# A two-layer transformer kernel: the order of its first stage, where its zero-fills start, and where the row that every token gets is added

## Chip, cores and metric

One NeuronCore of a Trainium2 chip runs the whole program. The metric is the time of one execution in microseconds (us) on the device; lower is better.

## What is computed

Two layers over x, 2 sequences of 2048 tokens with 256 features, in 32-bit floats. Layer 0, the part that the change touches, is

```
xn = layernorm(x)
x  = x + attention(xn, Wq,bq, Wk,bk, Wv,bv)        # causal, one head, softmax(q k^T / 16) v
       + shared(xn)                                # mean of 2 SwiGLU experts, biases sb1, sb2, sb3
       + routed(xn)                                # softmax gate (gate_w, gate_b), top 2 of 8 SwiGLU experts
```

Layer 1 has a second causal attention and a small 16-head block on the 256 highest-scoring tokens of each sequence. The change does not edit layer 1's computation.

Two facts carry the algebra at the start. The queries and keys are never formed separately: `wa` = Wq^T Wk is built once, and a score is xn · wa · xn^T plus terms from the biases. Of those, the key-side term is a vector `ca` added to the projected query, the query-side term is one number per row (`shift`) and bq·bk is one constant. Constants per row do not alter a softmax, but the kernel carries them. And the row `every` = (sb3[0]+sb3[1])/2 + bv is the same for all tokens, since the softmax weights sum to one and the shared experts are averaged.

## The kernel before

**Tiles.** Tokens lie in eight blocks of 512 (`x_blocks[g]`, 4 groups of 128 tokens). Blocks 0 to 3 are sequence 0. Attention goes over tiles of 128 queries, (0,0) to (0,15) upwards and then sequence 1 from tile 15 down. Tile i looks at i+1 groups of 128 keys, in chunks of up to 512.

**One attention tile.** `scores` (L251) multiplies on TensorE into PSUM; VectorE adds the mask (L260), adds the row shift and takes the maximum (L262, L268); ScalarE takes the exponential (L270). `turn` splits the row into two 16-bit planes on GpSimd (L301) and sends them through a transposing DMA on SP's queue (L303, `across`). `join` puts the halves together on VectorE (L281) and ScalarE (L282) as `pT`. `average` multiplies with the values (L316) and VectorE adds the result to x (L326). There are two `row` buffers, four each of `planes` and `across`, six `pT`, and two PSUM banks each for `sc`, `tr`, `mm`, `pv`.

**Work beside it.** A generator `side0` yields small steps that are woven between attention's pieces at a rate: `moments` (means and variances by L201, L202, and a reciprocal root by Newton steps, L185 to L190), `prepare0` (normalised rows on ScalarE, L223; transposes, L229, into `xnT`; 16-bit `rows` for the router, L472; the add of `every` to the block on GpSimd, L474; values, gate logits and shift in one product, L481), then the routing. `before_tile` forces steps until the tile's values exist, and issues zero-fills (`clear_some`, L420 onwards: scratch areas `sorted_x`, `sorted_y`, `gains`, 13 + 1 + 8 large DMAs, then biases) on ScalarE's queue. Before the first tile, the moments and `prepare0` of block 0 run whole.

**The beginning.** SP's queue loads all eight x blocks; ScalarE's queue loads wq, wk, bq, bk, wv, gate_w; GpSimd's queue loads gate_b and the three rows of `every`. TensorE turns wq and wk (L375), ScalarE copies them out (L376), then come ten products for the bias terms (L399, L404) and the four for `wa` (L457); `project_q0` (L594) makes a block's queries.

**Routed part.** 36 tiles of 256 sorted tokens. Per tile SP's queue loads the expert's w1, w2, w3 (`rw`, L684) and biases (`be`, L688) and a transposed `xs` (L693); GpSimd turns xs into `xT` (L698); TensorE does L705 into `sc` and `tr`, ScalarE and VectorE make `hid` (L713, L714, which need `be`), TensorE does L720 (needs w3), VectorE adds the bias (L725), SP stores (L726). Weights, `be` and `xs` have two buffers, `xT` three.

**What sets the order.** Each engine and each DMA queue works through its own list strictly in order. The lists are fixed beforehand by a planner that knows estimated durations; the code gives data dependencies and some order-only edges (`tc.add_manual_dep`). What a queue's front instruction waits for, everything behind it waits for as well.

Of the kernel before, what the change touches and what calls it, by code (L numbers as in the profile page):

```python
# [46 lines left out]
def transformer_kernel(ctx: ExitStack, tc: tile.TileContext, a: dict, out: bass.AP):  # L47
# [27 lines left out]
    for g in range(NB):  # L75
        load_x(g, nc.sync)
# [69 lines left out]
    def evacuate(dst, src):  # L146

        copies[0] += 1
        if copies[0] % 2:
            nc.vector.tensor_copy(dst, src)  # L150
        else:
            nc.scalar.copy(dst, src)

    def column(name, n, tag):
        t = const.tile([P, n], F32, tag=tag, name=tag)
        nc.scalar.dma_start(t, a[name])
        return t
# [35 lines left out]

    def moments(blocks):
# [3 lines left out]
        for k, g in enumerate(blocks):  # L198
            stats = small.tile([P, 4, 6], F32, tag="ln_stats", name="ln_stats")
            for j in range(4):  # L200
                nc.vector.bn_stats(stats[:, j, :], x_blocks[g][:, j, :])  # L201
                nc.vector.bn_aggr(mv[:, 4 * k + j, :], stats[:, j, :])  # L202
            if g != blocks[-1]:
                yield
# [11 lines left out]
    scaled = {}  # L216

    def layernorm(g, xn):

        xb = x_blocks[g]  # L220
        rstd, shift = scaled[g]
        for j in range(4):
            nc.scalar.activation(  # L223
                xn[:, j, :D], xb[:, j, :], AF.Identity, bias=shift[:, j : j + 1], scale=rstd[:, j : j + 1]
            )
        for c in range(2):
            ps = bank("mm")
            for j in range(4):
                nc.tensor.transpose(ps[:, j * P : (j + 1) * P], xn[:, j, c * P : (c + 1) * P], ident)  # L229
            evacuate(xnT[g][:, c, :], ps)  # L230
# [129 lines left out]
    with ExitStack() as l0:  # L360
# [6 lines left out]
        wq, wk = (work.tile([P, S], F32, tag="row", name=n)[:, : 2 * D].rearrange("p (c n) -> p c n", c=2)  # L367
                  for n in ("wq", "wk"))
        for dst, name in ((wq, "wq0"), (wk, "wk0")):
            turned = weight(work, name, "qT")  # L370
            ps = bank("mm")
            for ec in range(2):
                for dc in range(2):
                    k = (2 * ec + dc) * P
                    nc.tensor.transpose(ps[:, k : k + P], turned[:, dc, ec * P : (ec + 1) * P], ident)  # L375
            nc.scalar.copy(dst, ps.rearrange("p (c n) -> p c n", c=2))  # L376
        bq = column("bq0", 2, "bq0")
        bk = column("bk0", 2, "bk0")
        wvg = weight(wpool, "wv0", "wvg", cols=D + E + 1)
        nc.scalar.dma_start(wvg[:, :, D : D + E], a["gate_w"].rearrange("(c p) n -> p c n", p=P))  # L380
        gate_b = row_broadcast(wpool, ["gate_b"], "gate_b")


        every = wpool.tile([P, 1, D], F32, tag="every", name="every")
        parts = work.tile([P, 4, D], F32, tag="xn", name="parts", bufs=1)
        for k, src in enumerate((a["sb3"][0], a["sb3"][1], a["bv0"])):
            nc.gpsimd.dma_start(parts[:, k, :], src.partition_broadcast(P))
        nc.gpsimd.tensor_tensor(every[:, 0, :], parts[:, 0, :], parts[:, 1, :], ALU.add)
        nc.gpsimd.tensor_scalar(every[:, 0, :], every[:, 0, :], 0.5, None, op0=ALU.mult)
        nc.gpsimd.tensor_tensor(every[:, 0, :], every[:, 0, :], parts[:, 2, :], ALU.add)  # L390
        wa = wpool.tile([P, 2, D], F32, tag="wa", name="wa")
        ca = wpool.tile([P, 2], F32, tag="ca", name="ca")
        qk_bias = wpool.tile([P, 1], F32, tag="qk_bias", name="qk_bias")
        ps = bank("mm")
        for c in range(2):
            at = slice(c * P, (c + 1) * P)
            for k, (w, v) in enumerate(((wk, bq), (wq, bk))):
                for ec in range(2):
                    nc.tensor.matmul(  # L399
                        ps[:, 2 * k + c : 2 * k + c + 1], lhsT=w[:, ec, at], rhs=v[:, ec : ec + 1],  # L400
                        start=(ec == 0), stop=(ec == 1),
                    )
        for ec in range(2):
            nc.tensor.matmul(  # L404
                ps[:, 4:5], lhsT=bq[:, ec : ec + 1].to_broadcast([P, P]), rhs=bk[:, ec : ec + 1],
                start=(ec == 0), stop=(ec == 1),
            )
        nc.vector.tensor_scalar(ca, ps[:, 0:2], 1.0 / 16.0, None, op0=ALU.mult)
        nc.vector.tensor_scalar(wvg[:, :, D + E], ps[:, 2:4], 1.0 / 16.0, None, op0=ALU.mult)
        nc.vector.tensor_scalar(qk_bias, ps[:, 4:5], 1.0 / 16.0, None, op0=ALU.mult)  # L410

# [41 lines left out]

        for dc in range(2):
            ps = bank("mm")
            for ec in range(2):
                nc.tensor.matmul(  # L457
                    ps[:, :D], lhsT=wq[:, ec, dc * P : (dc + 1) * P], rhs=wk[:, ec, :],
                    start=(ec == 0), stop=(ec == 1),
                )  # L460
            evacuate(wa[:, dc, :], ps[:, :D])
        logits = plan.tile([P, NB * 4, E], F32, tag="logits", name="logits")
        rows, values, shifts = [None] * NB, [None] * NB, [None] * NB

        def prepare0(g):
# [3 lines left out]
            rows[g] = rows_pool.tile([P, 4, 2 * D], U16, tag=f"rows{g}", name=f"rows{g}")  # L469
            halves = xn.bitcast(U16).rearrange("p j (d k) -> p j d k", k=2)  # L470
            for k in range(2):
                nc.gpsimd.tensor_copy(rows[g][:, :, k * D : (k + 1) * D], halves[:, :, :, 1 - k])  # L472
            yield
            nc.gpsimd.tensor_tensor(  # L474
                x_blocks[g], x_blocks[g], every[:, 0:1, :].to_broadcast([P, 4, D]), ALU.add
            )
            vg = kv.tile([P, 4, D + E + 1], F32, tag=f"vg{g}", name=f"vg{g}")
            for j in range(4):
# [6 lines left out]
                evacuate(vg[:, j, :], ps[:, : D + E + 1])  # L485
                yield
            values[g] = vg
            shifts[g] = kv.tile([P, 4], F32, tag=f"shift{g}", name=f"shift{g}")
            nc.vector.tensor_scalar(shifts[g], vg[:, :, D + E], qk_bias, None, op0=ALU.add)
            nc.vector.tensor_tensor(  # L490
                logits[:, 4 * g : 4 * g + 4, :], vg[:, :, D : D + E],
                gate_b.unsqueeze(1).to_broadcast([P, 4, E]), ALU.add,
            )
# [107 lines left out]
        def side0():  # L601
            for blocks in (range(1, BPB), range(BPB, NB)):
                yield from moments(blocks)
                for g in blocks:
                    yield from prepare0(g)
# [3 lines left out]
        def before_tile(b, i):  # L609
            while values[b * BPB + i // 4] is None:  # L610
                step()
            rate[0] = BESIDE_L0[(values[BPB - 1] is not None) + (values[NB - 1] is not None)]
            if (b, i) > (0, 0):
                clear_some(2 if i < 8 and b == 0 else 1)

        for work_of in (moments([0]), prepare0(0)):
            for _ in work_of:
                pass
# [53 lines left out]
    with ExitStack() as moe:  # L672
# [55 lines left out]

        coming = later_weights()
        for t in range(LIKELY):  # L730
            product, activated = run(t)
            if t >= LIKELY // 3:
# [17 lines left out]
    ln1, ln2 = column("ln1", 2, "ln1"), column("ln2", 2, "ln2")  # L750
# [720 lines left out]
```

## Time and profile before

| what | us |
|---|---|
| three runs | 1544.1, 1547.49, 1548.82; median 1547.49 |
| profiled execution | 1543.37 |
| its span (first to last instruction) | 1541.7 |
| around the span | 1.67 |
| TensorE matmul busy | 1478.2 (96%) |
| VectorE, ScalarE, GpSimd busy | 697.3 (45%), 442.0 (29%), 410.2 (27%) |
| first score product | starts at 33.40 |
| first product with values | starts at 55.57 |
| routing's product L537 | starts at 131.97 |
| first routed product L705 | starts at 360.08 |

Stages: start and layer 0's attention to 360 us, routed experts to about 735, shared experts to about 1140 with the selected tokens of sequence 0 beside them, layer 1's attention to the end. TensorE's share says where the bound is, but not what a microsecond of one stage is worth: its busy time is modelled from starts and includes products that run at a lower clock. A gap in its list, or a stretch where the same product takes twice as long, is what can be won or lost.

### The profile page before, as it was taken

What the parts mean: (1) busy time and instruction counts of PE and PEld (TensorE: products, weight loads), DVE (VectorE), ACT (ScalarE), POOL (GpSimd) and SP (SyncE); (2) the same over time, 40 slices, a digit from 0 to 9 for tenths busy, and PEclk for the clock granted to TensorE, in tenths of its full rate; (3) what the DMA queues carried; (4) which work ended last, traced back from release to release, by engine and by line L of the source; (5) the groups of instructions that cost most, each with busy time, mean ns of one, the idle gap of its engine ahead of it and who ended that gap; (6) DMA issues with size and microseconds to landing.
All of it is one profiled execution on the core that took longest, in us unless ns stands there. A gap on an engine that the chain in (4) does not pass through costs nothing.

```text
span 1541.7 us, 17887 instructions
## 1 busy us (share of the span) xinstructions
PE 1478.2 (96%) x5828; PEld 1050.5 (68%) x5828; DVE 697.3 (45%) x2055; ACT 442.0 (29%) x831; POOL 410.2 (27%) x596
## 2 busy tenths in 40 slices
PE   7999899998999999999999999999999998999998
PEld 4566566567888888888565565566675765577665
DVE  6346333343222222222244445866546468666354
ACT  2443233242111111111112212114633532344233
POOL 3554577532111111110122210231003213421132
PEclk9899999999999999999999999999999999999999
DMA  4844556666879888965001110040004425621144
GB/s 152 255 109 120 135 139 138 149 138 150 209 215 226 239 234 256 261 189 158 28 28 41 42 34 21 28 150 18 11 11 92 115 67 106 165 57 23 29 119 102
DMA packets 290558, 183.49 MB, mean 119 GB/s; under 512 B 192960, under 2 KB 265408, under 8 KB 290464
## 3 DMA queue, kind: packets, MB, share of 16 engines
q1 hardware_dynamic: 255168, 134.95, 36.0%
q10 hardware_dynamic: 27664, 26.53, 5.6%
q0 software_dynamic: 7632, 20.86, 4.4%
q8 instruction: 47, 0.77, 0.2%
q14 instruction: 47, 0.39, 0.1%
HBM read 93.14 MB, written 45.14 MB: 90 GB/s over the span
## 4 chain that ended last, share of the span: by engine, by line
PE 28%; issue 10%; DVE 7%; POOL 3%; DMA 2%; ACT 2%; SPq 0%; POOLq 0%; ACTq 0%; DVEq 0%
PE ps_tr L1338 6%; PE ps_sc L1338 6%; PE ps_pv L1357 5%; POOL planes L301 3%; DMA across<-planes 2%; PE ps_mm L1209 1%; PE ps_mm L1171 1%; DVE x L1368 1%; PE ps_sc L251 1%; PE ps_mm L801 1%; PE ps_mm L1192 1%; PE ps_pv L316 1%; PE ps_mm L1275 1%; DVE row L262 1%; ACT pr L1183 1%
## 5 line engine op out<-in xcount | busy, mean ns | idle before, releaser
L301 POOL COPY planes<-row 128x512 uint16<-128x512 uint16 (+3 forms) x320 | 167.7, 569 | 306.8 <-ACT row L270 293.8
L282 ACT COPY pT<-across 128x512 uint16<-128x512 uint16 (+3 forms) x160 | 106.3, 677 | 226.9 <-DMA across<-planes 211.7
L251 PE MATMUL ps_sc<-xnT,qT 128*128 128x512 f32 (+3 forms) x384 | 161.2, 541 | 0.3 <-DVE qT L150 0.2
L714 DVE SCALAR_TENSOR_TENSOR hid<-ps_tr,be,act 128x256 f32<-128x256 f32 x144 | 63.0, 479 | 197.9 <-PE ps_tr L705 192.9
L713 ACT ACTIVATE act<-ps_sc,be 128x256 f32<-128x256 f32 x144 | 60.4, 470 | 302.1 <-PE ps_sc L705 302.1
L1327 POOL DMA_INDIRECT ya<-sorted_y,place x64 | 62.2, 973 | 318.0 <-DVE x L1368 224.9
L316 PE MATMUL ps_pv<-vg,pT 128*128 128x256 f32 x544 | 129.0, 390 | 12.4 <-ACT pT L282 12.0
L705 PE MATMUL ps_sc<-xT,rw 128*128 128x256 f32 x576 | 136.2, 379 | 1.6 <-POOL xT L698 1.6
L705 PE MATMUL ps_tr<-xT,rw 128*128 128x256 f32 x576 | 136.1, 379 | 0.0
L316 PE MATMUL ps_pv<-v,pT 128*128 128x256 f32 x544 | 128.4, 381 | 7.0 <-ACT pT L282 4.6
L720 PE MATMUL ps_pv<-rw,hid 128*128 128x256 f32 x576 | 132.0, 382 | 0.0
L698 POOL COPY xT<-xs 128x512 uint16<-128x512 uint16 x72 | 51.3, 758 | 299.8 <-issue 281.9
L316 PEld LDWEIGHTS ps_pv<-vg,pT 128*128 128x128 f32 x544 | 104.6, 195 | 37.6 <-ACT pT L282 17.5
L1338 PE MATMUL ps_sc<-xnT,sw 128*128 128x512 f32 x256 | 121.9, 594 | 0.1
L1338 PE MATMUL ps_tr<-xnT,sw 128*128 128x512 f32 x256 | 122.0, 593 | 0.0
L316 PEld LDWEIGHTS ps_pv<-v,pT 128*128 128x128 f32 x544 | 101.3, 190 | 29.1 <-ACT pT L282 7.9
L705 PEld LDWEIGHTS ps_sc<-xT,rw 128*128 128x128 f32 x576 | 109.4, 190 | 16.8 <-POOL xT L698 2.0
L705 PEld LDWEIGHTS ps_tr<-xT,rw 128*128 128x128 f32 x576 | 109.5, 190 | 14.8
L720 PEld LDWEIGHTS ps_pv<-rw,hid 128*128 128x128 f32 x576 | 105.0, 190 | 21.2 <-DVE hid L714 6.7
L1357 PE MATMUL ps_pv<-sw,hid 128*128 128x256 f32 x512 | 117.5, 380 | 0.0
L1357 PEld LDWEIGHTS ps_pv<-sw,hid 128*128 128x128 f32 x512 | 96.6, 190 | 18.7 <-issue 6.2
L281 DVE COPY pT<-across 128x512 uint16<-128x512 uint16 (+3 forms) x160 | 68.8, 436 | 89.2 <-DMA across<-planes 88.3
(319 smaller groups left out, 1936.7 us busy)
## 6 DMA issues: line engine op xcount, KB each, us to landing
rw<-in_rw SPq DMA_DIRECT2D x108, 512.0 KB, 4.6
sorted_x<-zero ACTq DMA_DIRECT2D x13, 768.0 KB, 6.6
sorted_y<-y SPq DMA_DIRECT2D x36, 256.0 KB, 4.8
be<-biases SPq DMA_DIRECT2D x36, 132.0 KB, 4.5
table<-xn SPq DMA_DIRECT2D x8, 514.0 KB, 3.7
x<-in_x SPq DMA_DIRECT2D x8, 512.0 KB, 6.8
gains<-zero ACTq DMA_DIRECT2D x8, 512.0 KB, 3.2
gain<-gains SPq DMA_DIRECT2D x16, 256.0 KB, 2.7
```

Source lines behind the costliest of these rows:

```text
L251: product = nc.tensor.matmul(ps[:, :w], lhsT=qT[:, dc, (i % 4) * P : (i % 4 + 1) * P], rhs=xnT[g0 + k][:, dc, :w], start=(dc == 0), stop=( ...
L281: nc.vector.tensor_copy(words[:, :, 1], flat[:, :w]),
L282: nc.scalar.copy(words[:, :, 0], flat[:, w : 2 * w]),
L301: nc.gpsimd.tensor_copy(planes[:, h * w : (h + 1) * w], halves[:, :, 1 - h])
L316: product = nc.tensor.matmul(pv[:, :D], lhsT=turned[k][:, j : j + P], rhs=values[g0 + k][:, j // P, :D], start=(c + j == 0), stop=(c + j = ...
L705: nc.tensor.matmul(ps[:, k * TT : (k + 1) * TT], lhsT=we_in[:, dc, (h + k) * P : (h + k + 1) * P], rhs=xT[:, dc, :], start=(dc == 0), stop ...
L713: activated = nc.scalar.activation(act, p1[:, at], AF.Silu, bias=b1[:, hc])
L714: nc.vector.scalar_tensor_tensor(hid[:, h + k, :], p2[:, at], b2[:, hc], act, op0=ALU.add, op1=ALU.mult)
L720: product = nc.tensor.matmul(po[:, r, :], lhsT=hid[:, hc, r * P : (r + 1) * P], rhs=w3[:, hc, :], start=(hc == 0), stop=(hc == 3),)
L1327: nc.gpsimd.indirect_dma_start(out=ya, out_offset=None, in_=sorted_y, in_offset=bass.IndirectOffsetOnAxis(ap=place[rank][:, t : t + 1], ax ...
L1338: product = nc.tensor.matmul(ps, lhsT=ww[:, dc, hc * P : (hc + 1) * P], rhs=xnT[g][:, dc, :], start=(dc == 0), stop=(dc == 1),)
L1357: product = nc.tensor.matmul(po[:, :D], lhsT=hid[:, hc, j * P : (j + 1) * P], rhs=w["sw3", n][:, hc, :], start=(hc == 0), stop=(hc == 3),)
```

## The change

It reorders the beginning. SP's queue loads block 0, then wk, then the other blocks; wq and wv go on ScalarE's queue, bk, bq and gate_b on GpSimd's (and layer 1's ln1, ln2). bk lands as a 257th column of the turned wk, so that the product `wa` yields the query-side bias column too. A tiny exponential is issued early on ScalarE. The first block's moments go ahead of the other blocks' on VectorE, and half of its normalised rows are made on VectorE. The ten bias products become five, behind `wa`. `gate_b` and bq·bk are added to the values' tail in place.

Block 0's values are no longer finished before the first tile: tile i waits for group i of its values only (`made`), so scores go between them. Other blocks' moments run as side steps that stay behind attention's own work. The zero-fills start at tile 4 (two per tile to tile 11, then one) in place of tile 1.

The add of `every` leaves `prepare0` (eight GpSimd instructions of 128x1024) and enters the routed part (32 of 128x256, written one per tile from tile 4), with its three loads and three small sums.

The core of the diff:

```diff
-    for g in range(NB):
-        load_x(g, nc.sync)
+    load_x(0, nc.sync)
...
             for j in range(4):
-                nc.vector.bn_stats(stats[:, j, :], x_blocks[g][:, j, :])
+                i = nc.vector.bn_stats(stats[:, j, :], x_blocks[g][:, j, :])
+                if first:
+                    tc.add_manual_dep(i.ins, first[0].name, order, reason="the first block's norm goes first")
                 nc.vector.bn_aggr(mv[:, 4 * k + j, :], stats[:, j, :])
+                if j == 1 and g >= BPB:
+                    yield HOLD
             if g != blocks[-1]:
-                yield
+                yield HOLD
...
+            if alone and j % 2:
+                nc.vector.tensor_scalar(
+                    xn[:, j, :D], xb[:, j, :], rstd[:, j : j + 1], shift[:, j : j + 1], op0=ALU.mult, op1=ALU.add
+                )
...
+        nc.gpsimd.dma_start(wk[:, :, D], a["bk0"])
+        bq = column("bq0", 2, "bq0", nc.gpsimd)
+        loaded = [weight(work, n, "qT", queue) for n, queue in (("wq0", nc.scalar), ("wk0", nc.sync))]
+        wvg = weight(wpool, "wv0", "wvg", cols=D + E + 1)
+        for g in range(1, NB):
+            load_x(g, nc.sync)
+
+        warm = const.tile([P, 1], F32, tag="warm", name="warm")
+        nc.vector.memset(warm, 0.0)
+        nc.scalar.activation(warm, warm, AF.Exp)
+        for _ in moments([0]):
+            pass
...
-        every = wpool.tile([P, 1, D], F32, tag="every", name="every")
-        parts = work.tile([P, 4, D], F32, tag="xn", name="parts", bufs=1)
-        for k, src in enumerate((a["sb3"][0], a["sb3"][1], a["bv0"])):
-            nc.gpsimd.dma_start(parts[:, k, :], src.partition_broadcast(P))
...
-                    ps[:, :D], lhsT=wq[:, ec, dc * P : (dc + 1) * P], rhs=wk[:, ec, :],
+                    ps[:, : D + 1], lhsT=wq[:, ec, dc * P : (dc + 1) * P], rhs=wk[:, ec, :],
...
             layernorm(g, xn)
-            rows[g] = rows_pool.tile([P, 4, 2 * D], U16, tag=f"rows{g}", name=f"rows{g}")
...
-            yield
-            nc.gpsimd.tensor_tensor(
-                x_blocks[g], x_blocks[g], every[:, 0:1, :].to_broadcast([P, 4, D]), ALU.add
-            )
...
         def side0():
-            for blocks in (range(1, BPB), range(BPB, NB)):
+            yield from prepare0(0)
+            for blocks in ((1,), (2, 3), range(BPB, NB)):
+                if blocks != (1,):
+                    yield HOLD
                 yield from moments(blocks)
...
         def before_tile(b, i):
-            while values[b * BPB + i // 4] is None:
+
+            while made[0] <= (NB * 4 - 1 if b else i):
                 step()
...
-            if (b, i) > (0, 0):
-                clear_some(2 if i < 8 and b == 0 else 1)
+            if (b, i) >= (0, 4):
+                clear_some(2 if (b, i) < (0, 12) else 1)
...
+        every = hp.tile([P, D], F32, tag="every", name="every", bufs=1)
+        parts = hp.tile([P, 2, D], F32, tag="parts", name="parts", bufs=1)
+        for dst, src in ((parts[:, 0, :], a["sb3"][0]), (parts[:, 1, :], a["sb3"][1]), (every, a["bv0"])):
+            nc.gpsimd.dma_start(dst, src.partition_broadcast(P))
+        nc.gpsimd.tensor_tensor(parts[:, 0, :], parts[:, 0, :], parts[:, 1, :], ALU.add)
+        nc.gpsimd.tensor_scalar(parts[:, 0, :], parts[:, 0, :], 0.5, None, op0=ALU.mult)
+        nc.gpsimd.tensor_tensor(every, every, parts[:, 0, :], ALU.add)
         coming = later_weights()
         for t in range(LIKELY):
             product, activated = run(t)
+            if 4 <= t < 4 + NB * 4:
+                xt = x_blocks[(t - 4) // 4][:, t % 4, :]
+                nc.gpsimd.tensor_tensor(xt, xt, every, ALU.add)
```

## Prediction

> **What bounds the kernel now.** First the busy row, then the slices of the page:
>
> ```profile
> PE 1478.2 (96%) x5828; PEld 1050.5 (68%) x5828; DVE 697.3 (45%) x2055; ACT 442.0 (29%) x831; POOL 410.2 (27%) x596
> ...
> PE   7999899998999999999999999999999998999998
> ```
>
> TensorE is the bound almost everywhere; its first slice of 38.5 us is the emptiest. An edit is worth what it does to gaps in TensorE's list or to its clock. The table by stage shows where both are bad:
>
> ```profile
> 33.40:55.57 22.17, 18.57 (x58) 9.97 (x56) 7.06 (x29) 7.81 (x19) 11.94 (x14) 0.77 0.89 270
> ```
>
> From the first score to the first product with values the granted clock is 0.77 and the DMA engines are 0.89 busy at 270 GB/s: six zero-fills of 768 KB were issued from 35.9 us on. The timeline of the beginning gives the causes:
>
> ```profile
> 13.78 0.43 DVE L201 BATCH_NORM_STATS2 ln_stats<-x 128x6 f32<-128x256 f32 x1 [3.52 <-DMA x<-in_x]
> ...
> 16.36 1.09 ACT L223 ACTIVATE xn<-x,ln_shift,ln_rstd 128x256 f32<-128x256 f32 x2 [5.12 <-DVE ln_shift L210]
> ...
> 24.20 2.34 POOL L474 TENSOR_TENSOR x<-x,every 128x1024 f32<-128x1024 f32 x1
> 24.34 2.23 DVE L189 SCALAR_TENSOR_TENSOR rs_t<-rs_t,ln_var 128x12 f32<-128x12 f32 x1
> ...
> 33.40 0.82 PE L251 MATMUL ps_sc<-xnT,qT 128*128 128x128 f32 x4
> ...
> 49.20 6.53 PE L594 MATMUL ps_mm<-xnT,wa 128*128 128x512 f32 x8 [0.57 <-DVE xnT L150]
> ...
> 55.57 0.59 PE L316 MATMUL ps_pv<-vg,pT 128*128 128x256 f32 x2
> ```
>
> VectorE's list mixes block 0's norm with statistics of block 2, and stops 3.52 us for that load; so the normalised rows start at 16.36. L189, normally 0.17 us, takes 2.23 and ends with GpSimd's L474. At 49.2 eight query products take 6.53 us where they took 3.6 at 29.96.
>
> The routed part's start:
>
> ```profile
> 360.08 1.99 PE L705 MATMUL ps_sc<-xT,rw 128*128 128x256 f32 x8 [1.59 <-POOL xT L698]
> ...
> 368.83 1.23 SPq L693 DMA_TRANSPOSE xs<-sorted_x  x1
> ...
> 370.79 0.37 SPq L684 DMA_DIRECT2D rw<-in_rw  x1
> ...
> 372.83 0.35 SPq L688 DMA_DIRECT2D be<-biases  x1
> ```
>
> TensorE waits for GpSimd's first xT. SP's list has the order xs(5), w3(2), be(2): behind xs(5), which waits for xT(3) to free its buffer, stand two loads that tile 2 needs.
>
> **The Trainium skill.** "TensorE: Matmul & The Clock Gate", Part 1: the array runs at half rate until it has been busy for a window of about 3.4 us, and again after an idle one. The trace agrees on the factor (L594 0.592 us at its fastest, 1.219 at its slowest), and 3.69 us of idling ahead of 162.16 is followed by 24 value products in 8.11 us, where 24 full-rate starts at 0.215 take 5.2. "SBUF — State Buffer", section on the two separate sides: VectorE with two SBUF inputs and GpSimd exclude each other for a whole instruction; L189 above agrees. "Trainium Kernel Development and Optimization", Key Constraints: the queues of SP, ScalarE and GpSimd share the 16 DMA engines; moving a load between queues changes its order, not the bandwidth. The trace shows queues only, so it neither confirms nor denies this.
>
> **The beginning, step by step** (times from the trace before; TensorE takes two starts per 32-bit product).
> 1. Norm: statistics of block 0 start at 5.47 as before and take 1.7; then 13 dependent small steps at a pitch of 0.21 (L185 to L210 at 31 to 33.6 us): shift ready near 10, not 16.27.
> 2. Weights: wk moves to SP behind block 0; it landed at 8.5 and should land at 7 to 8.5. Its copy also waits for bk on GpSimd's queue, issued at 2.3; the loads there took 7.3 to land, so 8 to 10.5. ScalarE's table load (1.28 at 8.87) is gone from the path. I take wk ready at 10.8, against 11.2: almost nothing.
> 3. `wa`: eight starts at 0.51 (2.05 for four at 15.57): 15.0. Bias products: ten starts in place of twenty that took 4.4: 17.2. Three tiny evictions stand ahead of the transposes' bank: 18. Transposes 2.0 and evictions 0.7: 20.8. Group 0's values 1.0, queries 3.4 warm or 6.8 cold; half and half 4.9: the first score at **26.7**, against 33.4. Three groups of values (2.7) are then still to do, so this is worth 4.0.
> 4. Scores 0 to 3, those values, block 1's transposes and values, and half its queries are 13.1 us of full-rate starts. Before, 13.0 took 22.2. The waits named there go: no zero-fill before tile 4, no L474 on GpSimd (one held planes and then L262 for 1.42), a warm clock. Next in line is VectorE: block 1's statistics and root steps (2.2 + 2.7) now sit between evictions. I find about 0.8 of waits for evictions; first value product at 40.6. It has 2.6 less behind it (block 2's transposes 0.9, half of block 1's queries 1.7): 55.57 - 40.6 - 2.6 = **12.4 gained**. Bounds: cold queries and 4 us of VectorE in front of evictions leave 6.4; full clock by 22 gives 14.
>
> **From there to the routing** the trace before loses 5 of 76 us. About 19 us of statistics and root steps of blocks 2 to 7 (six blocks at 2.2, two groups of 13 steps at 2.7) move from VectorE's idle start into this stretch, where it is 52% busy; all 13 `sorted_x` fills now fall on tiles 4 to 10, but fills at tiles 4 to 7 caused no wait for `pT` before. **2 lost**, bounds -1 and 6. ln1, ln2 and gate_b on another queue land long before use: nothing; their cover is hundreds of us for ln, 15 for gate_b.
>
> **Start of the routed part.** The compiled order of the changed kernel does not spread the adds. GpSimd's list there reads: three loads (parts, every), xT(0), xT(1), three small sums, 5 adds, xT(2), 17 adds, xT(3), 10 adds, xT(4) and on. Rows that price it:
>
> ```profile
> L474 POOL TENSOR_TENSOR x<-x,every 128x1024 f32<-128x1024 f32 x8 | 18.8, 2353 | 5.2 <-DVE row L262 5.2
> ...
> L387 POOL DMA_DIRECT2D parts<-in_sb x2 | 1.1, 552 | 0.0
> ...
> L390 POOL TENSOR_TENSOR every<-every,parts 128x256 f32<-128x256 f32 x1 | 0.7, 721 | 0.1
> ```
>
> The loads wait for attention's last products, as xT(0) did at 358.61: 3 x 0.54 = **1.6** ahead of xT(0), straight onto the path (nothing if the buffer is free earlier). Count from xT(0)'s start; TensorE begins at 1.5, tile 2 at 22.4 (10.4 per tile), its L720 at 29.4. With a us per add: xT(0), xT(1) 2.8; sums 2.9; 5a; xT(2) 1.45; 17a; xT(3) 1.45: done at 8.6 + 22a. be(2) is issued 3.3 to 4.0 behind xs(5) (382.54 - 379.24, 372.83 - 368.83; I take 3.65) and lands after 4.5; ScalarE and VectorE need 1.05 for the first `hid`. TensorE's wait is 17.8 + 22a - 29.4 = 22a - 11.6. With a = 0.70 (between 2.353/4 = 0.59 and 0.72): **3.8**. Bounds: a = 0.59 gives 1.4; a = 0.85 (pitch of the dependent sums) 7.1, plus 2.9 of cold clock. Tile 3's be, reckoned the same way, comes some 2 us before it decides; the rest of the adds are covered by 8.98 us of idle GpSimd per tile.
>
> Removed with it: 18.8 us of GpSimd beside attention, counted in step 4; later GpSimd has slack except at 150 to 300 us, where nothing changes.
>
> **The rest.** Layer 1's list is planned anew; its compiled order differs though its code doesn't. TensorE idles some 28 us after 1000. No reason for a sign: 0, bounds -4 and 4.
>
> **Sum**: -12.4 + 2 + 1.6 + 3.8 + 0 = **-5.0**. Against the profiled execution (span 1541.7, 1543.37 with what lies around it): 1538.4. That execution lies 4.1 under the runs' median of 1547.5; from the median, **1542.5**.
>
> **Rivals.**
> - *The adds decide (slower).* GpSimd's 22 adds ahead of xT(3) hold SP's queue so long that TensorE goes cold: 1.6 + 7.1 + 2.9 = 11.6, against a front gain at its low end, 6.4 - 2 = 4.4 net: +7; with the front between, +5: **1552.5**. From a = 0.82 on with a cold clock the loss exceeds the front's 10.4. For it: no cover at SP, the list is strict. Against it: L474's price per element is lower.
> - *The front is given back (no change).* bk lands late, queries run cold, VectorE's statistics delay evictions: 6.4 - 2 gained, 5.4 lost: +1 to -1; **1547**. For it: TensorE stayed cold until about 27 us before, though busy from 11.
> - *The loads of `parts` need not wait*, and a stays near 0.6: -12.4 + 2 + 1.6 = -9, **1538.5**; part of "faster".
>
> **Chances.** A measurement of this kernel can tell 0.3%, 4.6 us. Faster 0.46 (the sum and the third rival), same 0.30, slower 0.24. The likeliest case alone: 1536 to 1546; to hold 8 in 10 the range takes in both others: 1532 to 1553.
>
> **What would show it.** Right: first score near 27 and first value product near 41; L594's second group at about 0.43 a start; GpSimd gives TensorE its first xT some 3.2 us after the last value product; tile 2's L720 waits 2 to 6 us with xT(3) late. Wrong: first value product after 48; or tile 2 without a wait; or adds under 0.55 or over 0.8 us.

## The result, and the profile after

The changed kernel takes 1561.89 us (median of 4 runs, 1557.10 to 1567.80), the kernel before 1545.80 beside it (4 runs, 1538.44 to 1548.82): ratio **1.0119, 95% interval 1.0081 to 1.0157**. The prediction said 1542.5, with 1553 as its upper end: it had the wrong sign. Its profiled execution took 1557.16 with a span of 1555.5, so it is one of its faster ones. First the busy row of the page after and the slices of TensorE:

```profile
PE 1479.0 (95%) x5818; PEld 1052.2 (68%) x5818; DVE 712.4 (46%) x2075; ACT 442.1 (28%) x830; POOL 414.2 (27%) x626
...
PE   7899899889999999999999999999999899899988
```

TensorE is as busy as before (1479.0 against 1478.2 us) in a span that is 13.8 us longer. No work was added to it; what was added is gaps and cold products. So the next thing is to cut the span at events that both kernels have, from the timeline of TensorE:

| stretch (profiled executions) | before | after | difference |
|---|---|---|---|
| start to the end of the last product of layer 0's attention | 358.48 | 349.07 | -9.4 |
| from there to the first product of the shared experts | 380.26 | 385.39 | +5.1 |
| to the first score of layer 1 | 425.15 | 425.43 | +0.3 |
| layer 1, first score to the end of the last product | 373.03 | 390.61 | **+17.6** |
| rest of the span | 4.8 | 5.0 | +0.2 |

The loss is in layer 1, some 800 us after the end of the attention that was edited. The beginning is much faster than before. The table by stage, from first score to first product with values:

```profile
20.23:34.53 14.30, 13.91 (x58) 9.04 (x57) 11.04 (x46) 7.29 (x19) 7.33 (x12) 1.00 0.37 84
```

Where it was 22.17 us at a clock of 0.77 with the DMA engines 0.89 busy, it is 14.30 us at full clock with the DMA engines 0.37 busy. The timeline of the beginning (start, duration, engine, line, operation, idle before it):

```profile
9.00 3.80 PE L455 MATMUL ps_mm<-wk,wq 128*128 128x257 f32 x8 [1.26 <-ACT wk L402]
...
9.72 0.16 DVE L214 SCALAR_TENSOR_TENSOR ln_shift<-ln_mv,ln_rstd 128x4 f32<-128x4 f32 x1
...
16.80 3.60 PE L608 MATMUL ps_mm<-xnT,wa 128*128 128x512 f32 x8
...
20.23 0.38 PE L266 MATMUL ps_sc<-xnT,qT 128*128 128x128 f32 x2
...
34.53 0.59 PE L331 MATMUL ps_pv<-vg,pT 128*128 128x256 f32 x2
```

`wa` starts at 9.00, shift is ready at 9.9, the queries run at full rate (eight in 3.60 us), the first score stands at 20.23 and the first product with values at 34.53. At the other end, layer 1. The waits of TensorE between 1320 and 1370 us, before:

```profile
PE ps_mm L1109 <- ACT part L152: 1.7, 1, 1.7
PE ps_mm L1192 <- ACT pr L1183: 1.1, 1, 1.1
PE ps_mm L1087 <- DVE part L150: 0.5, 1, 0.5
PE ps_mm L1171 <- DVE vs L150: 0.2, 1, 0.2
```

and after:

```profile
PE ps_mm L1029 <- DMA across<-planes: 5.2, 1, 5.2
PE ps_mm L1155 <- DVE turn L1150: 4.2, 1, 4.2
```

3.5 us of small waits have become 9.4 us in two. The first is put down to a DMA; the timeline shows who it was:

```profile
1332.33 0.95 POOL L1071 DMA_INDIRECT rows<-in_mask,at_row  x1 [0.31 <-issue]
...
1333.03 4.76 DVE L188 SCALAR_TENSOR_TENSOR rs_y<-rs_t,rs_y 128x2 f32<-128x2 f32 x1
1333.28 4.49 POOL L316 COPY planes<-row 128x512 uint16<-128x512 uint16 x8
...
1338.46 0.61 DVE L1049 TENSOR_SCALAR hn<-chosen,rms_rs 128x256 f32<-128x256 f32 x2
...
1339.01 1.09 PE L1029 MATMUL ps_mm<-ident,hn 128*128 128x128 f32 x4 [5.20 <-DMA across<-planes]
```

VectorE's L188, two columns of a Newton step that take 0.16 us elsewhere, takes 4.76: it begins while GpSimd is at an indirect DMA, and ends with the eight `planes` copies behind it. Behind it in VectorE's list stands `hn` (L1049), and TensorE waits for that; the DMA was merely the last event ahead. The same happens at 1357:

```profile
1356.79 0.95 POOL L1125 DMA_INDIRECT cols<-turned,at_col  x1 [0.30 <-issue]
...
1357.45 4.87 DVE L1149 TENSOR_TENSOR turn<-turn,side 128x256 f32<-128x256 f32 x1
1357.75 4.28 POOL L316 COPY planes<-row 128x512 uint16<-128x512 uint16 x8
...
1362.79 1.09 PE L1155 MATMUL ps_mm<-ident,turn 128*128 128x128 f32 x4 [4.18 <-DVE turn L1150]
```

In the kernel before, VectorE is through with the root 0.45 us before the copies start (timelines of VectorE and of GpSimd):

```profile
1332.55 0.15 DVE L190 SCALAR_TENSOR_TENSOR rms_rs<-rs_t,rs_y 128x2 f32<-128x2 f32 x1
```

```profile
1333.15 4.58 POOL L301 COPY planes<-row 128x512 uint16<-128x512 uint16 x8 [5.47 <-issue]
```

The Trainium skill ("SBUF — State Buffer", section on the two separate sides) has the rule: a VectorE operation with two SBUF inputs and a GpSimd operation that reads SBUF exclude each other. L188 and L1149 have two SBUF inputs, and the copies read SBUF, so the trace agrees. After each of the two stalls TensorE runs cold; the table by stage gives 0.89 and 0.83 where the kernel before has 1.00:

```profile
1340.00:1360.00 20.00, 18.61 (x71) 13.07 (x70) 12.59 (x34) 7.62 (x11) 4.17 (x7) 0.89 0.41 106
1360.00:1380.00 20.00, 17.21 (x64) 12.64 (x65) 11.86 (x26) 4.79 (x10) 2.93 (x6) 0.83 0.26 49
```

### The profile page after: what moved, and what is told of

Its sections match the earlier page's. It is cut to its first block, busy times and chain, and to the rows that moved or that the text cites. A ratio compares the mean times of both kernels' runs of the same rounds, so it can differ in the third digit from the quotient of the medians.

```text
span 1555.5 us, 17929 instructions
## 1 busy us (share of the span) xinstructions
PE 1479.0 (95%) x5818; PEld 1052.2 (68%) x5818; DVE 712.4 (46%) x2075; ACT 442.1 (28%) x830; POOL 414.2 (27%) x626
## 4 chain that ended last, share of the span: by engine, by line
PE 33%; DVE 8%; issue 6%; POOL 2%; DMA 2%; ACT 1%; POOLq 0%; ACTq 0%; DVEq 0%
PE ps_tr L1365 6%; PE ps_sc L1365 6%; PE ps_pv L1384 5%; PE ps_pv L331 2%; PE ps_sc L266 2%; POOL planes L316 2%; PE ps_mm L828 2%; DMA across<-planes 2%; PE ps_mm L1236 2%; PE ps_mm L1198 1%; PE ps_tr L266 1%; DVE x L1395 1%; PE ps_mm L1414 1%; PE ps_mm L1219 1%; PE ps_mm L1290 1%
## 5 line engine op out<-in xcount | busy, mean ns | idle before, releaser
L331 PE MATMUL ps_pv<-vg,pT 128*128 128x256 f32 x544 | 130.2, 391 | 18.3 <-ACT pT L297 13.8
L331 PE MATMUL ps_pv<-v,pT 128*128 128x256 f32 x544 | 132.8, 389 | 8.4 <-DVE nmx L283 3.8
L1384 PEld LDWEIGHTS ps_pv<-sw,hid 128*128 128x128 f32 x512 | 96.4, 190 | 18.4 <-issue 4.8
L266 PEld LDWEIGHTS ps_sc<-xnT,qT 128*128 128x128 f32 x384 | 70.2, 190 | 54.4 <-issue 43.1
```

The lines of the kernel that those rows point to most:

```text
L266: product = nc.tensor.matmul(ps[:, :w], lhsT=qT[:, dc, (i % 4) * P : (i % 4 + 1) * P], rhs=xnT[g0 + k][:, dc, :w], start=(dc == 0), stop=( ...
L331: product = nc.tensor.matmul(pv[:, :D], lhsT=turned[k][:, j : j + P], rhs=values[g0 + k][:, j // P, :D], start=(c + j == 0), stop=(c + j = ...
L1384: product = nc.tensor.matmul(po[:, :D], lhsT=hid[:, hc, j * P : (j + 1) * P], rhs=w["sw3", n][:, hc, :], start=(hc == 0), stop=(hc == 3),)
```

## The experiments

**What moved layer 1?** `side1(b)`, the chain that normalises a sequence, selects 256 tokens and runs the 16-head block, calls the same generator `moments` as layer 0. The change put new yields into it. For blocks 4 to 7 that is one HOLD in the middle of each block, four more steps, and a HOLD in place of three plain yields. What follows a HOLD is tied behind attention's own work: 14 of the 16 statistics of sequence 1, which the planner had placed between 971 and 1163 us, now run in one bunch at 1198.6 to 1206.5. So the order of layer 1 did not change by chance.

The theory was that this pin costs the time. The rivals were the four steps by themselves, the residue of the pacing credit (the fraction of a step that is left over when steps are dealt out to attention's pieces; 0.64 in the kernel before at the start of the shared experts, 0.48 in the changed one), and something carried over from the routed part. Four kernels:

```diff
 # e1, from the changed kernel: layer 0 keeps the new yields, layer 1 steps as before
-                if j == 1 and g >= BPB:
+                if j == 1 and g >= BPB and in0[0]:
                     yield HOLD
...
-                yield HOLD
+                yield HOLD if in0[0] else None
 # e2: all yields stay, but plain ones in layer 1 (this line, and the HOLD between blocks)
-                    yield HOLD
+                    yield HOLD if in0[0] else None
 # e3: e1, and ahead of the shared experts
+    credit[0] = 0.64
 # e4, from the kernel before: e1's condition turned round
+                if j == 1 and g >= BPB and not in0[0]:
+                    yield HOLD
```

> The changed kernel, but with the new yields in `moments` (a HOLD after the second group of a block, a HOLD between blocks) used in layer 0 alone; layer 1 steps as before. Theory 1 (the shared `moments` generator pins sequence 1's statistics behind attention's own VectorE work in layer 1; the 16 pairs at 1198 to 1207 us go back to between 1000 and 1165): ratio to the kernel before 0.994 to 1.000, that is some 12 to 18 us faster than the changed kernel. Rival A (layer 1's order is disturbed by the residue of the step pacing alone): 1.008 to 1.016, as the changed kernel. Rival B (the adds of `every` or the throttle in the routed part carry over): 1.008 to 1.016.

> The changed kernel with all its yields kept, but plain ones in place of HOLD when layer 1 calls `moments`: the planner may place the statistics early, the side chain keeps its four additional steps. If the pin (HOLD) costs the time: 0.994 to 1.002. If the four more steps, which put sequence 1's routing 3.2 pieces later, cost it: 1.008 to 1.016. In between if both do.

> As the first of these, and the pacing credit set to 0.64 ahead of the shared experts, the value it has in the kernel before (0.48 in the changed one), so that layer 1's code is issued in the same order as before. Theory 1: within 0.3% of the first of these, 0.993 to 1.000. Rival A: the credit is what matters, 0.993 to 1.000 here, but 1.008 or more in the first of these.

> The kernel before with only layer 1's `moments` stepping as in the changed kernel (HOLDs and four more steps); layer 0 is untouched. Theory 1: 1.008 to 1.016 slower, the statistics in one bunch beside the first tiles of layer 1's attention. Rivals A and B: 0.998 to 1.003.

| run | ratio to before, interval | layer 1, us (profile) |
|---|---|---|
| changed kernel | 1.0119, 1.0081 to 1.0157 | 390.6 |
| e1 | 1.0039, 1.0021 to 1.0058 | 374.1 |
| e2 | 1.0149, 1.0115 to 1.0184 | 390.8 |
| e3 | 1.0024, 1.0012 to 1.0036 | 374.9 |
| e4 | 1.0076, 1.0054 to 1.0098 | 388.5 |

e1 and e4 put the cost into `moments` in layer 1, and the rivals of a carry-over and of the credit alone fall. Neither number is quite where theory 1 put it: e1 stays above its 0.994 to 1.000 (what is left is in the other stages, see below), and e4 is just under its 1.008. But **e2 overturned my theory of the pin**: with the statistics free to go early (and they went early), the four more steps cost all of it. The same two stalls stand in e2's trace, 4.75 and 4.79 us long. That leaves the place of the chain beside attention's tiles.

**Is it the place of the chain, and do the stalls make the time?** Four more:

```diff
 # e5, from the changed kernel (e8: the same line in the kernel before)
     rate[0] = BESIDE_L1
+    credit[0] += 4.0
 # e6, from the changed kernel: rmsnorm's root column by column, one SBUF tensor each; `side` in PSUM
+                    nc.vector.tensor_scalar(t[:, c], y[:, c], y[:, c], None, op0=ALU.mult)
...
-            side = fp.tile([P, 64, 8], F32, tag="qm", name="side", bufs=2)
+            side = bank("mm").rearrange("p (n d) -> p n d", d=8)
 # e7, from the kernel before: four empty steps at the head of side1(1)
+            if b:
+                yield from quiet(4)
```

> The changed kernel with all its HOLDs and steps, and the pacing credit raised by 4 at the start of layer 1's attention: the four additional steps are taken at once, and the chain of sequence 1 (statistics, selection, 16-head block) stands beside the same tiles as in the kernel before. If the chain's place is the cause: 1.000 to 1.006, and no VectorE instruction of 4 us or more beside a run of `planes` copies. If the HOLD or the bunch of statistics at 1198 to 1206 us is: 1.010 to 1.017.

> The changed kernel, its chain as late as it is, with the two instructions that took 4.8 us (the root's L188 in rmsnorm, the `turn` difference L1149) in forms that read one tensor from SBUF: the root's products as tensor-by-column-scalar, one column at a time, and `side` in PSUM. If the exclusion of VectorE and GpSimd is what turns lateness into time: both waits of TensorE (5.2 and 4.2 us) go and the cold clock behind them, 1.000 to 1.006. If the stalls are only where a late chain happens to wait and the time is lost elsewhere: 1.009 to 1.016. If a column scalar is excluded as well: one of the two stalls stays, 1.004 to 1.012.

> The kernel before, layer 0 and `moments` untouched, with four empty steps at the head of sequence 1's chain in layer 1. If the chain's place is the cause: 1.007 to 1.016. If it needs the rest of the change as well: 0.998 to 1.003.

> The kernel before with the pacing credit raised by 4 at the start of layer 1's attention: the same chain four steps early. If only lateness costs: 0.995 to 1.003. If the place of the chain was fitted to the tiles and any shift costs: 1.005 to 1.016.

| run | ratio to before, interval | layer 1, us |
|---|---|---|
| e5 | 1.0023, 1.0009 to 1.0038 | 376.9 |
| e6 | 1.0041, 1.0029 to 1.0052 | 381.7 |
| e7 | 1.0042, 1.0023 to 1.0061 | 384.1 |
| e8 | 1.0066, 1.0045 to 1.0087 | 386.1 |

e5 keeps every HOLD and every step, takes the four at once, and the loss is gone. e7 and e8 shift the chain in the otherwise untouched kernel, and both cost, late and early. So the place was fitted to the tiles: a chain four steps off loses 11 to 18 us of layer 1 in these profiles, in either direction. One profile of layer 1 isn't exact: the same order took 373.0 in the kernel before and 377.9 in e12 below. The late and early ones lie above both. Over the runs e7 costs less than its profile says: 1.0042 is some 6.5 us, below the 1.007 to 1.016 that I had expected.

e6 shows what the stalls make of it in the changed kernel: with the chain still late, 9.0 us of layer 1's 17.6 come back in the profile, and over the runs the ratio falls from 1.0119 to 1.0041, though 3.5 of the first wait's 5.2 us are left. That stall moved on to `hn`, by the timelines of VectorE and GpSimd:

```profile
1339.52 0.33 DVE L191 TENSOR_SCALAR rms_rs<-rs_t,rs_y 128x1 f32<-128x1 f32 x2
1339.76 3.83 DVE L1057 TENSOR_SCALAR hn<-chosen,rms_rs 128x256 f32<-128x256 f32 x2
```

```profile
1337.74 0.95 POOL L1079 DMA_INDIRECT rows<-in_mask,at_row  x1 [0.31 <-issue]
1338.69 4.49 POOL L324 COPY planes<-row 128x512 uint16<-128x512 uint16 x8
```

The column-wise steps pass beside the copies at 0.17 us each; the 128x256 product of one SBUF tensor behind them (0.61 for two, before) takes 3.83. The second stall, with `side` in PSUM, is gone: TensorE's wait there is 0.6.

But the stalls are not the only way in which a shifted chain costs time. No stall of over 4 us stands in e4, e7 or e8. The longest that GpSimd's copies hold a VectorE instruction of layer 1 there is 1.75 us in e4 and 2.33 in e7, with no wait of TensorE over 1.1 us beside it, and nothing comparable in e8; yet layer 1 is 15.5, 11.0 and 13.1 us longer than in the kernel before. TensorE's waits there are others: none over 2.8 us in e4 and e7, and two of 5.4 and 4.0 us ahead of the products of `hn` in e8. So the place of the chain is shown to be the cause; the held VectorE is shown to be part of how it costs in the changed kernel, and how it costs in the other three was not taken apart.

**What do the moved adds cost?** Two kernels from e5:

```diff
 # e9: loads and small sums behind the first xT, each add behind its own tile's xT
+                after_xT(nc.gpsimd.tensor_tensor(xt, xt, every, ALU.add))
 # e10: the add back in prepare0
+            nc.gpsimd.tensor_tensor(
+                x_blocks[g], x_blocks[g], every[:, 0:1, :].to_broadcast([P, 4, D]), ALU.add
+            )
```

> The kernel of e5 (changed kernel, chain put back) with the adds of `every` tied behind the xT of their own routed tile, one per tile, and the three loads and small sums placed behind the first xT. Everything after the routed part is in the same order as in e5. If the bunched adds and the loads cost what e5's trace shows at the start of the routed part (the wait for the first xT 3.73 us where it was 1.59, and the cold products behind it): wait near 1.6, routed part 378.7 us as before and not 381.3, ratio 0.998 to 1.001, where e5 had 1.0023. If the adds cost something later in the routed part in any order: 1.001 to 1.004.

> The kernel of e5 with the add of `every` back beside attention, eight adds of 128x1024 on GpSimd, and the row built at the beginning as in the kernel before. Undoes that part of the change alone. If GpSimd has room beside attention: routed part as before, 4.9 us won, 0.998 to 1.001. If 18.8 us of GpSimd work and the exclusion of VectorE cost more in attention than in the routed part: attention ends 5 us or more later, 1.002 to 1.007.

e9: **0.9984** (0.9971 to 0.9997). From the last product of attention to the first shared one it takes 380.24 us, as before (380.26); e5 takes 385.01. TensorE's wait for the first xT:

```profile
353.51 1.99 PE L727 MATMUL ps_sc<-xT,rw 128*128 128x256 f32 x8 [1.59 <-POOL xT L720]
```

against the changed kernel's, where the next products are cold as well (the first 16 take 5.99 us, 3.56 before):

```profile
352.81 3.78 PE L720 MATMUL ps_sc<-xT,rw 128*128 128x256 f32 x8 [3.73 <-POOL xT L713]
356.38 2.58 PE L720 MATMUL ps_tr<-xT,rw 128*128 128x256 f32 x8
...
383.59 3.72 PE L735 MATMUL ps_pv<-rw,hid 128*128 128x256 f32 x16 [0.35 <-DVE hid L729]
```

e10: 1.0062 (1.0038 to 1.0086). The routed part is cured too (380.23), but attention ends at 364.17 instead of 353.23 and layer 1's order moved with it (382.1). VectorE is held up there again: L515, 0.2 us elsewhere, takes 2.26 at 54.50. With the new beginning, taking the adds out of attention is worth about 11 us in these two profiles, and what moved into the routed part gave 5 of these back. Most of the 5 is not the bunch of adds. In the changed kernel the three loads of the row stand on GpSimd's list ahead of the first xT, from 349.64 to 351.30; the longer wait behind them (2.14 us) and the cold products behind the wait (2.43) make 4.6. The adds come after that xT, and all that shows of them on TensorE is the 0.35 above. e9 moved loads and adds at once, so this division is read from the trace and not from a run.

**Where does the beginning's gain go?** At the first product with values the changed kernel is 21.0 us ahead with 2.6 us more work left, at the end of attention 9.4. With the 2.6 taken off that is 9.0 lost; in e1, e2, e3, e5 and e6, whose layer 0 is the same, it is 10 to 14. (Profiles of one and the same layer 0 differ. Eight with the new one have the first product with values at 34.0 to 38.0 us and the end of attention at 349.1 to 355.8; four with the old one have 52.3 to 55.6 and 353.5 to 358.5. A difference of 3 us between two single profiles says little.) Three waits of TensorE are there, near 70, 105 and 167 us:

```profile
72.67 3.78 PE L331 MATMUL ps_pv<-vg,pT 128*128 128x256 f32 x8 [4.50 <-DVE rs_t L187]
...
105.60 0.71 PE L489 MATMUL ps_mm<-wvg,xnT 128*128 128x265 f32 x2 [2.22 <-DVE xnT L149]
...
166.96 3.29 PE L331 MATMUL ps_pv<-vg,pT 128*128 128x256 f32 x7 [4.90 <-ACT pT L297]
```

Six kernels tried a cause each. e11 (from e5) leaves out the statistics of blocks 1 to 7, e12 (from the kernel before) has only the later fills, e13 (from e9) cuts the fills into halves, one per piece, e15 (from e9) fills from tile 1, e16 and e17 join later. e14 is the changed kernel with the edits of e3 and e9 together.

```diff
 # e11, in moments
+        if in0[0] and first:
...
+                scaled[g] = same[:, 0, 4 * k : 4 * k + 4], same[:, 1, 4 * k : 4 * k + 4]
+            return
 # e12; e15 is the reverse
-            if (b, i) > (0, 0):
-                clear_some(2 if i < 8 and b == 0 else 1)
+            if (b, i) >= (0, 4):
+                clear_some(2 if (b, i) < (0, 12) else 1)
 # e13, for sorted_x and sorted_y; tiles 2 to 11
-            step = 3 * TT
+            step = 3 * TT // 2
...
             pieces[0] += 1
+            if filling[0]:
+                fill_hook[0](1)
 # e16; in e17 with 2
-                joins.append((pieces[0] + LAG + k, k, w, across, turned))
+                lag = LAG + 1 * (shifts is not None and b == 0)
+                joins.append((pieces[0] + lag + k, k, w, across, turned))
```

> The kernel of e5 without the statistics and root steps of blocks 1 to 7 in layer 0 (their rows are not normalised: scale 1, shift 0, part of the computation left out); steps and holds stay. If these steps on VectorE give the beginning's gain back between tiles 3 and 10: the wait of 4.5 us near 68 to 73 us for the root and the cold clock behind it go, and the lead over the kernel before at the end of tile 10, 6.9 us in e5, becomes 12 to 16. If the values, transposes and zero-fills that are packed into these tiles do it: the lead stays between 5 and 9.

> The kernel before with only the zero-fills moved to tile 4 and on. Everything after layer 0 is in the same order as in the kernel before. If the fills cause the cold clock and the full DMA engines between 33 and 56 us: the first score stays at 33.4, the first product with values comes at 45 to 50 instead of 52 to 56. If it is the VectorE and GpSimd work there: 52 to 56. Time over all: 0.996 to 1.001 in the first case, since part is given back by the fills later; 0.999 to 1.003 in the second.

> The kernel of e9 with the same bytes of zero-fill cut into halves, issued one at a time along the pieces of tiles 2 to 11 instead of in pairs ahead of a tile. If pairs of 768 KB fills hold up the transposing DMA `across` (in the changed kernel it landed 5.6 us after its issue at 64.28, and VectorE and TensorE waited) and so give the beginning's gain back: the 4.5 us wait near 68 to 73 us shrinks to under 2 and attention ends with a lead over the kernel before 3 to 6 us larger than the 6.6 us of e9. If not: a lead of 5 to 8 us. Layer 1's order may move with it, so the end of attention is what is read.

> The changed kernel with the adds spread as in e9, and layer 1 stepped and paced as in the kernel before (e3). Beginning and routed part as in e9, layer 1 between 374 and 375 us, where e9 took 377.4 from its first score to its last product: 0.996 to 0.999. If each of the parts measured before doesn't add up: 0.999 to 1.003.

> The kernel of e9 with the zero-fills from tile 1 as in the kernel before; everything after layer 0 in the same order as in e9. If the fills lose less at the beginning than beside tiles 4 to 10: 0.995 to 0.998. If their place there makes the changed beginning slow as in the kernel before: first product with values 3 to 8 us later than e9's 36.2, and 0.998 to 1.002 over all.

> The kernel of e14 with the joins of sequence 0 in layer 0 one piece later (LAG 6 in place of 5), so that VectorE and ScalarE reach a `pT` copy later in their lists; everything after layer 0 in the same order as in e14. If VectorE's standing in front of `pT` copies whose transposing DMA hasn't landed (2.3 us near 73, 2.3 near 107 in e14), with evictions and the root behind it, is what gives the beginning's gain back: the TensorE waits of 4.5 and 2.25 us shrink to under 3 together and attention ends 3 to 6 us earlier than e14's 353.2 us; ratio 0.993 to 0.996. If TensorE needs that `pT` itself by then, the wait only changes its name: attention ends within 2 us of e14's or later, 0.995 to 1.000.

> As the one before, two pieces later (LAG 7). If standing in front of `pT` copies is the cause: as good or better, 0.992 to 0.996. If TensorE needs the `pT`: worse than one piece, 0.997 to 1.003, with more waits of TensorE for ScalarE's and VectorE's `pT` copies.

| run | ratio to before, interval | first value product | lead at the end of tile 8 (its add to x) | end of attention |
|---|---|---|---|---|
| before | 1 | 55.57 | 0 | 358.48 |
| e5 | 1.0023, 1.0009 to 1.0038 | 37.68 | 12.3 | 353.23 |
| e9 | 0.9984, 0.9971 to 0.9997 | 36.22 | 11.8 | 351.92 |
| e11 | 1.0039, 1.0024 to 1.0053 | 35.10 | 16.3 | 349.33 |
| e12 | 0.9992, 0.9980 to 1.0003 | 49.24 | 4.6 | 355.58 |
| e13 | 0.9993, 0.9981 to 1.0005 | 37.97 | 5.8 | 357.67 |
| **e14** | **0.9968**, 0.9952 to 0.9984 | 37.96 | 12.0 | 353.15 |
| e15 | 0.9991, 0.9977 to 1.0005 | 41.43 | 5.9 | 352.68 |
| e16 | 1.0016, 1.0003 to 1.0029 | 37.75 | 8.0 | 360.52 |
| e17 | 1.0018, 1.0002 to 1.0033 | 35.94 | 16.3 | 360.31 |

- e11: without the statistics the three waits are still there (4.63, 2.24, 5.66 us). Its lead falls by 4.2 us from tile 0 to tile 8 where e5's falls by 5.4: the statistics are 1 to 2 us of the loss. At tile 10 the lead is 10.9, between the two ranges that I had set (5 to 9, and 12 to 16). The time over all did not fall.
- e12: the fills alone explain 3 to 6 of the 21 us at the first value product (49.24, where four profiles with the fills from tile 1 have 52.3 to 55.6). At the end of attention nothing is left that stands clear of these four.
- e13 and e15: neither the pairing nor the place of the fills is the cause. With half fills the first wait is still 4.49 us, with fills from tile 1 it is 4.37. e15 has its first value product 5.2 us later than e9 and ends attention within 1 us of it. That the fills cost about as much wherever they stand is my reading; single profiles don't show it to 3 us.
- e16, e17: both are slower than e14, and e16 lies above both ranges that I had given it. e17 takes the first wait away (4.5 becomes 0.94) and is 16.3 us ahead at tile 8. Then it loses all of it in one wait, by TensorE's timeline:

```profile
172.59 0.76 ACT L298 COPY pT<-across 128x512 uint16<-128x512 uint16 x1 [18.84 <-DMA across<-planes]
...
173.41 2.93 PE L333 MATMUL ps_pv<-vg,pT 128*128 128x256 f32 x6 [12.99 <-ACT pT L298]
```

Ahead of it GpSimd's list has eleven scatters of rows (`sorted_x`, the first at 142.68, a pitch of 1.27 us) in front of the `planes` of that tile, which run from 156.47 to 160.32; its transposes are issued from 169.19 on. What stood in front of these on SP's list are loads of a register, with which the routed part fetches the expert of each of its tiles (`tile_expert`, 36 in all, at a pitch of 0.56 us or more). The view of their line, in e17 and then in the changed kernel from 149 to 163 us (count; ns at least, median, at most; first and last start):

```profile
L701 SPq TENSOR_LOAD <-tile_expert x26: 3/262/941, 145.6 to 168.5; - x26
```

```profile
L692 SPq TENSOR_LOAD <-tile_expert x19: 262/265/945, 150.0 to 162.0; - x19
```

In the changed kernel the `planes` run from 156.76, and the transposes start at 162.69, right behind the last of the 19 loads and 5 us behind the first two copies; TensorE's wait of 4.90 us up to 166.96 follows. The kernel before has 14 such loads up to 156.47, transposes at 156.51, and a wait of 3.69 up to 162.16. So by the traces most of the third wait comes from SP's list, in both kernels; no run moved these loads.

The first scatter stands at 142.23 in the kernel before and at 140.96 in the changed one: **the routing did not come earlier although the beginning did**. The loads can't start before the routing has written their table. My reading is that this stretch takes what is ahead of it. No run moved the routing, the scatters or the loads alone, so how the loss divides between them stays open, and so does the cause of the first two waits.

e14 adds up what was learned, and is faster than both kernels, than the kernel before by 0.3%: 1541.17 us against 1545.34 (0.9968). It keeps the new beginning, the new place of the adds and the later fills.

## Why the prediction was wrong, point by point

- **The step that failed is "The rest".** It said of layer 1 that "its compiled order differs though its code doesn't", and put 0 with bounds of 4. The premise was false: `moments` and its new yields run in layer 1 too, so that the change leaves layer 1's arithmetic alone, but not its order. It measured +17.6, and the experiments put this down to sequence 1's chain standing four steps late. The lines were in the diff I had read; I counted `moments` for layer 0 alone.
- **Beginning, 12.4 gained.** Right in kind, low in size. First score 20.23, predicted 26.7; first value product 34.53, predicted 40.6. With the 2.6 us of work left behind it that is 18.4 gained, above the upper bound of 14. (Eight profiles with this layer 0 against four with the old one give 15.6 on the mean, still above it.) Shift came at 9.9 as reckoned (about 10). The 6.5 us to the first score are: `wa` started at 9.00 and not 10.8; it took 3.6, not 4.2; bias products and small evictions took 1.8, not 3.0 (transposes at 14.39); and from there to the score it was 5.8, not 8.7, the queries being warm where I took them half cold. From first score to first value product, 14.3 against 13.9, the size was right. One reading was off: eight zero-fills, not six, were issued between 35.9 us and the first value product.
- **From first value product to routing, 2 lost.** The term was mis-sized: 9.0 lost to the end of attention in this trace, 10 to 14 in others of the same layer 0. The cause I named, VectorE's statistics, is 1 to 2 of it (e11), and the term had no wait for SP's list in it. Together the two misses nearly cancel: 9.4 ahead at the end of attention in the profile, where I had 10.4. That the sum fits is luck.
- **Start of the routed part, 1.6 + 3.8.** Right in sum, 5.1 against 5.4, by luck; e9 shows that it is these adds and loads together. Wrong in parts. The loads took 1.66 us, and the wait grew by 2.14; but what followed was 2.43 us of cold products, and tile 2's wait was 0.35, not 3.8, below the 2 to 6 that were to show the prediction right. The adds took 0.69 each, as reckoned (0.70), and the fourth xT came 23.2 us after the first (24.0); TensorE was itself late by the cold products, and be(2) was issued 2.6 us behind xs(5), not 3.65.
- **Rivals.** "The adds decide" ended on the right side, at 1552.5, for a reason that did not happen: tile 2 hardly waited. "The front is given back" happened in part, not by bk, cold queries or evictions as it said.
- **The sum.** -9.4 + 5.1 is -4.3, close to the -5.0 predicted for all but layer 1. Over several profiles the end of attention is nearer to 3.5 us early (mean of six with this layer 0, 352.7, against four with the old, 356.2), so without the loss in layer 1 the change would still be a little slower. e1, e3 and e5 agree (1.0023 to 1.0039).

## What to carry to other kernels

When a diff touches a helper, list every caller before pricing it; a yield in a generator that is woven between other work is a shift of everything behind it. In a schedule that was tuned by hand, "moved by four steps" needs a price of its own: one place to look is what runs within a microsecond of another engine that excludes it, here VectorE's root 0.45 us ahead of GpSimd's copies; but the same shift cost 11 us and more where nothing of the kind happened. And a gain early in the program is only worth what is left of it behind the next point where something else sets the time. A DMA queue's list holds more than DMAs: here register loads stood in front of transposes that TensorE waited for.

## What the runs showed of the hardware

The exclusion of VectorE and GpSimd does not always end with one instruction. Where a run of `planes` copies followed an idle GpSimd, VectorE operations with two SBUF inputs went in between, one for one: 0.58 us for L1071 at 1333.29 in the kernel before, whose eight copies took 4.58. Where the run stood directly behind an indirect DMA of GpSimd, VectorE was held to its end in five cases: 4.76 and 4.87 us in the changed kernel, 4.75 and 4.79 in e2, 3.83 in e6, beside runs of copies of 4.49 us or less. The first four are operations with two SBUF inputs; the fifth, `hn`, reads one SBUF tensor. Two conversions of one small SBUF tensor (128x2, 0.15 us in the kernel before) were held there too, but ended half a us before the run did: 2.33 us at 1338.01 in e7, 1.75 at 1346.55 in e4. Beside all other runs of four or more copies, in all 19 traces, no VectorE operation with two SBUF inputs took over 1.56 us (over 500 of them). The Trainium skill's page ("SBUF — State Buffer", same section) has the lock last for an instruction; here it lasted for a run. Why an indirect DMA ahead makes the difference is open.
